# Selective scans on one core: the first of four states scanned in PSUM and multiplied there by VectorE, the other three by GpSimd a step later

## The chip, the core and the metric

The kernel runs on 1 core of one Trainium2 chip. It uses the core's five engines: TensorE (PE in the profile; PEld is its loading of weights), VectorE (DVE), ScalarE (ACT), GpSimd (POOL) and SyncE (SP, which here only issues DMAs). Each engine works through its own queue in order and waits on semaphores that the others raise. VectorE, ScalarE and GpSimd read and write SBUF; VectorE and ScalarE also read and write PSUM, the banks that TensorE writes.

The metric is device time in microseconds. Before the change it was 11,709.09 us, the median of 3 runs (11,697.75 to 11,709.36).

## The reference, cut to what matters

The program is four layers over 4 images of 64 x 64 positions with 96 channels. Layers 0 and 1 are Mamba-like blocks: each image is read in four orders, and along each order a selective scan runs for every channel and each of 16 states. Layer 1 does this on a half spectrum (33 x 64 positions, Fourier transforms around it). Layers 2 and 3 are attention without softmax and a quantized feed-forward network on the tokens. What the change touches is the scan:

```
def step(hst, inputs):
    ul, dl, bl, cl = inputs
    dA = jnp.exp(dl[..., None] * A)
    hst = hst * dA + (dl * ul)[..., None] * bl[:, :, None, :]
    y = jnp.einsum('bkdn,bkn->bkd', hst, cl)
    return (hst, y)
```

So for each channel d and state n, along the sequence l: `h[l] = exp(delta[l] * A[n]) * h[l-1] + delta[l] * u[l] * B[n, l]`, and `y[l]` is the sum over the 16 states of `h[n, l] * C[n, l]`.

## The kernel before, in words

The scans are one long loop, written out by hand in `scans` (line 480): the kernel's text is the order of the instructions on PE, VectorE, ScalarE and GpSimd. There are six phases: two of layer 0 (two images each) and four of layer 1 (one image each). A phase has four directions, a direction is cut into segments of the sequence (eight of 512 in layer 0; 512, 512, 384, 384 and 320 in layer 1), 144 segments in all. A segment has 4 groups of states (`q`, four states each) times 3 chunks of 128 channels (`c`): 12 steps, 1,728 in all. A step treats 128 channels on the partitions, S positions along the free axis, and four states, of which 0 and 1 are called x and 2 and 3 are called y.

For a step the loop (lines 763 to 828) needs:
- the factors `exp(delta * A)` of four states, by ScalarE (line 635): of the x states into SBUF (`ax`), of the y states into a PSUM bank (`ay`, from `room`);
- the inputs `delta * u * B`. For the x states ScalarE makes them transposed, piece by piece, well ahead (`make_bx`, line 600), and TensorE transposes them into a PSUM bank (`px`, line 630). For the y states GpSimd multiplies `du` by the broadcast B into the SBUF tile `hy` (`front_b`, line 653), which has one buffer;
- four scans by VectorE (`scan`, line 660): x from SBUF and PSUM into the SBUF tile `hx`, y from PSUM and SBUF in place in `hy`;
- the products with C, two states at a time: GpSimd makes `hcx` (line 805), VectorE makes `hcy` (line 822);
- the last column of each state, copied into `state` for the next segment (`keep_state`, line 673): of x by GpSimd, of y by ScalarE (by GpSimd when ScalarE has a long burst);
- the sum over states: TensorE transposes the products into the accumulating bank `acc` (`accumulate`, line 682), two states at a time; after the last group ScalarE copies `acc` out and SP stores it (`close_chunk`, line 709).

Three PSUM banks with the tag `ab` serve `px` and `ay` in rotation, in the order in which `room` is called. B and C come as rows of a DRAM tensor `xd`, broadcast over the partitions by DMAs on SP's queue (`broadcast`, line 580; `fetch` gets one group `q` ahead, at `c == 0`): C in two tiles of two states with four buffers, B in one tile of two states with two buffers. In layer 0 each tile takes two DMAs, one per image.

Other work is threaded through the steps. `prepare` makes `delta`, `du` (line 560, one VectorE product of three chunks per segment), the transposes and `xd` for the next segment; an environment `E` works off side tasks of the other layers: projections with TensorE, flips with GpSimd (line 306), normalization and gating (line 440 is a VectorE product with two SBUF operands), tokens and their feed-forward network (lines 1133, 1211, 1230, 1234 on VectorE). Both advance in the `slot` calls, three a step; pieces marked `LATE` (mostly those with VectorE work) only in the last one, and long ScalarE pieces, marked `BURST`, only in `burst`.

## Time and profile before

| what | value | where from |
|---|---|---|
| median of 3 runs | 11,709.09 us | times |
| profiled execution: span | 11,704.4 us | head of the page (the page gives no other time of that execution) |
| before the first scan, after the last | 215 us, 396 us | timeline: the first scan starts at 215.5, the last ends at 11,308.3 |
| VectorE, ScalarE, GpSimd, PE busy | 90%, 78%, 76%, 79% | page, part 1 |
| four scans of a step of 512 | 4.8 us | timeline, start to start |
| `hcy`, 1024 elements | 1.311 us mean | groups by shape |
| `hcx`, 1024 / 768 / 640 elements | 2.363 / 1.818 / 1.545 us mean | groups by shape |
| one product of `front_b`, 512 / 384 / 320 | 1.272 / 0.999 / 0.862 us mean | groups by shape |
| state copy on GpSimd, two columns | 0.850 us mean | groups |
| DMA queues busy, mean over 16 engines | 45.5% | page, part 3 |

A row of a timeline reads: start and duration in us, engine, line of the kernel, operation, tiles written and read, shapes, and how many like it are merged; in brackets, how long the engine sat idle before it and what ended that. In rows of windows, each engine has its busy time in us and its number of instructions; the last three columns are the granted TensorE clock, the DMA engines' busy share and GB/s. Tile names lose their trailing digits, so `ab_l`, `b_l` and `_l` name the rotating PSUM banks.

### The profile page before, as it was taken

The numbers are of one execution on the slowest core, as the hardware profiler recorded it, in microseconds if no ns is written. First come the engines' busy times: TensorE is split into PE (matmuls) and PEld (weight loads), VectorE is DVE, ScalarE is ACT, GpSimd is POOL, SyncE is SP. The second block draws the span as 40 slices with busy tenths as digits, with TensorE's granted clock in tenths as the row PEclk, the third lists the DMA queues.
The fourth block names the chain that finished last, engine by engine and source line by source line (L and its number), as shares of the span: only waits on it lengthen the run. The fifth ranks groups of instructions, "written<-read, shape, count | busy, mean of one in ns | idle before, by whom it ended". The sixth has DMA issues, their size and how long they took to land. (4 is left out here: it accounts for less than half of the span.)

```text
span 11704.4 us, 164864 instructions
## 1 busy us (share of the span) xinstructions
PE 9301.7 (79%) x54800; PEld 6722.3 (57%) x54800; DVE 10549.4 (90%) x10183; ACT 9089.0 (78%) x18533; POOL 8931.5 (76%) x7075
## 2 busy tenths in 40 slices
PE   6678888787888878877888888888778877788765
PEld 3455555555666556555665565565556655565554
DVE  6899999999999998999888989988999999899974
ACT  3778888898888888887767878877787787777753
POOL 2889999887887897897768878877767767677640
PEclk8789999988988998998889989988879988898887
DMA  5454454555555445445544353454225432443242
GB/s 145 120 142 119 126 127 115 141 155 158 153 153 129 124 124 141 120 127 162 153 129 124 114 147 120 142 150 119 88 79 158 122 96 92 124 137 106 83 117 42
DMA packets 1270879, 1469.07 MB, mean 126 GB/s; under 512 B 496071, under 2 KB 1033871, under 8 KB 1260679
## 3 DMA queue, kind: packets, MB, share of 16 engines
q1 hardware_dynamic: 1270023, 1458.53, 45.5%
q8 instruction: 430, 7.05, 0.3%
q14 instruction: 426, 3.49, 0.1%
HBM read 1221.74 MB, written 236.50 MB: 125 GB/s over the span
## 5 line engine op out<-in xcount | busy, mean ns | idle before, releaser
L653 POOL TENSOR_TENSOR hy_l<-du_l,bc_l 128x512 f32<-128x512 f32 (+2 forms) x3456 | 3957.3, 1166 | 1934.8 <-DVE hcy_l L822 960.1
L805 POOL TENSOR_TENSOR hcx_l<-hx_l,bc_l 128x1024 f32<-128x1024 f32 (+2 forms) x1617 | 3525.5, 2180 | 239.1 <-DVE hx_l L660 197.9
L600 ACT ACTIVATE bx_l<-dut_l,bt_l 128x192 f32<-128x192 f32 (+2 forms) x6272 | 2793.7, 498 | 0.0
L682 PE MATMUL acc_l<-ident,hcx_l 128*128 128x128 f32 (+1 forms) x12006 | 1876.0, 305 | 392.6 <-POOL hcx_l L805 388.4
L635 ACT ACTIVATE ax_l<-delta_l,l_alog 128x512 f32<-128x512 f32 (+2 forms) x3456 | 2139.1, 667 | 0.0
L682 PE MATMUL acc_l<-ident,hcy_l 128*128 128x128 f32 (+1 forms) x12000 | 1841.9, 302 | 302.4 <-DVE hcy_l L822 299.0
L682 PEld LDWEIGHTS acc_l<-ident,hcy_l 128*128 128x128 f32 (+1 forms) x12000 | 1551.5, 155 | 859.2 <-DVE hcy_l L822 475.7
L682 PEld LDWEIGHTS acc_l<-ident,hcx_l 128*128 128x128 f32 (+1 forms) x12006 | 1526.4, 156 | 861.5 <-POOL hcx_l L805 665.9
L822 DVE TENSOR_TENSOR hcy_l<-hy_l,bc_l 128x1024 f32<-128x1024 f32 (+2 forms) x1616 | 1951.1, 1207 | 43.6
L660 DVE TENSOR_TENSOR_SCAN hx_l<-ax_l,state_l,b_l 128x512 f32<-128x512 f32 (+2 forms) x1650 | 1787.4, 1124 | 212.7 <-PE b_l L630 136.9
L660 DVE TENSOR_TENSOR_SCAN hy_l<-b_l,state_l,hy_l 128x512 f32<-128x512 f32 (+2 forms) x1649 | 1782.9, 1118 | 89.3 <-ACT b_l L635 81.4
L635 ACT ACTIVATE b_l<-delta_l,l_alog 128x512 f32<-128x512 f32 (+2 forms) x1913 | 1196.6, 628 | 627.6 <-DVE hx_l L660 599.0
L630 PE MATMUL b_l<-ident,bx_l 128*128 128x128 f32 (+1 forms) x6724 | 1169.6, 302 | 363.0 <-DVE hy_l L660 203.5
L635 ACT ACTIVATE ab_l<-delta_l,l_alog 128x512 f32<-128x512 f32 x1321 | 907.1, 689 | 547.5 <-DVE hx_l L660 496.4
L630 PEld LDWEIGHTS b_l<-ident,bx_l 128*128 128x128 f32 (+1 forms) x6724 | 827.1, 152 | 861.3 <-DVE hy_l L660 337.1
L660 DVE TENSOR_TENSOR_SCAN hy_l<-ab_l,state_l,hy_l 128x512 f32<-128x512 f32 x961 | 1172.1, 1257 | 60.8 <-POOL hy_l L653 31.9
L660 DVE TENSOR_TENSOR_SCAN hx_l<-ax_l,state_l,ab_l 128x512 f32<-128x512 f32 x962 | 1176.5, 1263 | 49.3 <-PE ab_l L630 27.3
L630 PE MATMUL ab_l<-ident,bx_l 128*128 128x128 f32 x5288 | 889.1, 305 | 383.2 <-DVE hy_l L660 206.3
L673 POOL COPY state_l<-hx_l 128x2 f32<-128x2 f32 x1344 | 1141.9, 850 | 0.0
L630 PEld LDWEIGHTS ab_l<-ident,bx_l 128*128 128x128 f32 x5288 | 652.0, 154 | 715.6 <-DVE hy_l L660 326.6
L274 PE MATMUL pc_l<-pad_l,l_dg 128*128 128x512 f32 (+2 forms) x1656 | 787.9, 564 | 56.0 <-ACT uh_l L252 46.6
L176 PE MATMUL pi_l<-xi_l,l_wi 96*128 96x384 f32 (+6 forms) x912 | 458.6, 619 | 180.0 <-ACT zh_l L342 60.4
(225 smaller groups left out, 11821.3 us busy)
## 6 DMA issues: line engine op xcount, KB each, us to landing
bc_l<-l_xd_l SPq DMA_DIRECT2D x1536, 256.0 KB
bc_l<-l_xd_l SPq DMA_DIRECT2D x384, 512.0 KB
bc_l<-l_xd_l SPq DMA_DIRECT2D x384, 384.0 KB
us_l<-l_u SPq DMA_DIRECT2D x96, 768.0 KB
l_y<-y_l SPq DMA_DIRECT2D x288, 256.0 KB
bc_l<-l_xd_l SPq DMA_DIRECT2D x192, 320.0 KB
yt_l<-l_y SPq DMA_DIRECT2D x264, 192.0 KB
yt_l<-l_y SPq DMA_DIRECT2D x128, 384.0 KB
```

The lines of the kernel that those rows point to most:

```text
L176: self.nc.tensor.matmul(out[i * cfg.PI : (i + 1) * cfg.PI, :n], wi[:, ki, half, :], xin[:, max(i, ki), :n], start=(ki == 0), stop=(ki == c ...
L274: nc.tensor.matmul(pc[:, : n * 64].rearrange("p (r w) -> p r w", w=64), diag[:, t, :], pad[:, r - p0 + dy : r - p0 + dy + n, dx : dx + 64] ...
L600: nc.scalar.activation(t[:n, b, :, ch], z.dut[:n, b, :, ch], AF.Copy, scale=z.bt[:n, b, m : m + 1])
L630: nc.tensor.transpose(pb[:, t : t + n], st.z.bx[st.q, j][:n, b, st.c], ident[:n, :n])
L635: nc.scalar.activation(out, z.delta[:, st.c, : z.S], AF.Exp, scale=z.blk.A[:, st.c, z.k, n : n + 1])
L653: nc.gpsimd.tensor_tensor(st.hy[:, j, :S], st.z.du[:, st.c, :S], st.z.b[st.q][:, j, :S], ALU.mult)
L660: nc.vector.tensor_tensor_scan(h[:, j, : z.S][:, ::step], a[:, : z.S][:, ::step], b[:, : z.S][:, ::step], 0.0 if z.first else z.state[st.c ...
L673: copy(z.state[st.c][:, n0 : n0 + 2].rearrange("p (j o) -> p j o", o=1), h[:, :, e : e + 1])
L682: nc.tensor.matmul(z.acc[st.c][:n, b, :], hc[:, j, t : t + n], ident, start=(n0 + j == 0 and b == 0), stop=(n0 + j == NST - 1 and b == 0), ...
L805: nc.gpsimd.tensor_tensor(hcx[:, :, :S], hx[:, :, :S], z.c[q][0][:, :, :S], ALU.mult)
L822: nc.vector.tensor_tensor(hcy[:, :, :S], st.hy[:, :, :S], z.c[q][1][:, :, :S], ALU.mult)
```

## The change

A step keeps its four scans, but the results go to other places and the products are shared out differently.
- State 0 is scanned in place in its PSUM bank `px[0]`. VectorE multiplies it with C right after, from PSUM into a new SBUF tile `hk` (512 elements); ScalarE copies its last column from PSUM; TensorE adds it to `acc` in the same step (`multiply_kept`).
- States 1, 2 and 3 are scanned into one SBUF tile `h` of three rows with three buffers. In the next step, GpSimd copies their last columns (one copy of three) and multiplies all three rows by C in place (`multiply`); TensorE adds them to `acc` in that next step, behind its transposes for the step after (`add_rest`).
- `hcx`, `hcy`, `hx` and `hy` go. `front_b` for the next step now stands in GpSimd's queue behind `multiply` for the previous one.
- The exponentials of states 2 and 3 are both issued within their own step, so that the PSUM banks rotate in another order.
- B is fetched at `c == 0` as before; C is fetched at `c == 1` instead, as one tile of four rows with two buffers (the same bytes in half the DMAs).
- `acc` is taken when its first product comes, `close_chunk` runs one step later, and a new phase's side tasks are added at its third step instead of its first.

```
+        self.kept = 1
+        self.px, self.ay = {}, {}
...
-        t = sp.tile([P, 2, SM], F32, name=f"bc{what}_{z.nm}_{n}", tag=f"bc{what}", bufs=2 + 2 * what)
+        t = sp.tile([P, many, SM], F32, name=f"bc{what}_{z.nm}_{n}", tag=f"bc{what}", bufs=2)
...
-    def fetch(z, q):
-        z.c[q] = [broadcast(z, 4 * q + 2 * j, 1) for j in range(2)]
-        z.b[q] = broadcast(z, 4 * q + 2, 0)
+    def fetch_b(z, q):
+        z.b[q] = broadcast(z, 4 * q + 2, 2, 0)
+
+    def fetch_c(z, q):
+        z.c[q] = broadcast(z, 4 * q, 4, 1)
...
-        st.hy = sp.tile([P, 2, SM], F32, name=f"hy_{st.nm}", tag="hy")
+        st.h = sp.tile([P, 3, SM], F32, name=f"h_{st.nm}", tag="h", bufs=3)
...
-    def scan(st, h, j, a, b, n):
+    def scan(st, j):
         z = st.z
-        step = -1 if z.rev else 1
+        S, step, n = z.S, -1 if z.rev else 1, 4 * st.q + j
+        h = st.px[j][:, :S] if j < st.kept else st.h[:, j - 1, :S]
+        a = st.ax[:, j, :S] if j < 2 else st.ay[j][:, :S]
+        b = st.px[j][:, :S] if j < 2 else h
...
+    def multiply_kept(st, j):
+
         z = st.z
+        n = 4 * st.q + j
+        hk = sp.tile([P, SM], F32, name=f"hk_{st.nm}_{j}", tag="hk", bufs=2)
+        nc.vector.tensor_tensor(hk[:, : z.S], st.px[j][:, : z.S], z.c[st.q][:, j, : z.S], ALU.mult)
         if not z.last:
+            e = last(z)
+            nc.scalar.copy(z.state[st.c][:, n : n + 1], st.px[j][:, e : e + 1])
+        accumulate(st, hk, n)
+
+    def multiply(st):
+
+        z = st.z
+        lo, n = st.kept - 1, 4 * st.q
+        h = st.h[:, lo:, : z.S]
+        if not z.last:
+            e = last(z)
+            nc.gpsimd.tensor_copy(
+                z.state[st.c][:, n + st.kept : n + 4].rearrange("p (j o) -> p j o", o=1), h[:, :, e : e + 1]
             )
+        nc.gpsimd.tensor_tensor(h, h, z.c[st.q][:, st.kept :, : z.S], ALU.mult)
...
+    def add_rest(st):
+        for j in range(st.kept, 4):
+            accumulate(st, st.h[:, j - 1], 4 * st.q + j)
...
-            hx = sp.tile([P, 2, SM], F32, name=f"hx_{st.nm}", tag="hx")
-            scan(st, hx, 0, st.ax[:, 0], st.px[0], 4 * q)
-            front_y(st, 1)
+            if c == 1:
+                if q + 1 < NQ:
+                    fetch_c(z, q + 1)
+                elif after:
+                    fetch_c(after, 0)
+            scan(st, 0)
+            front_y(st, 2)
             if nxt:
-                nxt.ay = {}
                 front_x(nxt)
+            multiply_kept(st, 0)
+            front_y(st, 3)
             long = burst()
-            scan(st, hx, 1, st.ax[:, 1], st.px[1], 4 * q + 1)
+            if before:
+                multiply(before)
+            if nxt:
+                front_b(nxt)
             slot(None)
+            scan(st, 1)
...
-                nxt.px = [transposed(nxt, 0)]
-            hcx = sp.tile([P, 2, SM], F32, name=f"hcx_{st.nm}", tag="hcx", bufs=2)
-            nc.gpsimd.tensor_tensor(hcx[:, :, :S], hx[:, :, :S], z.c[q][0][:, :, :S], ALU.mult)
-            keep_state(nc.gpsimd.tensor_copy, st, hx, 4 * q)
+                transposed(nxt, 0)
             more.take(skip=long)
-            scan(st, st.hy, 0, st.ay[0], st.hy[:, 0], 4 * q + 2)
+            scan(st, 2)
+            slot(None, hold=long)
             if nxt:
-                nxt.px.append(transposed(nxt, 1))
-            slot(None, hold=long)
-            scan(st, st.hy, 1, st.ay[1], st.hy[:, 1], 4 * q + 3)
-            keep_state(nc.gpsimd.tensor_copy if long else nc.scalar.copy, st, st.hy, 4 * q + 2)
-            if nxt:
-                front_y(nxt, 0)
-            more.take(skip=long and c == C - 1)
+                transposed(nxt, 1)
             if closing:
                 close_chunk(closing)
-            accumulate(st, hcx, 4 * q)
+            closing = None
+            if before:
+                add_rest(before)
+                closing = before if before.q == NQ - 1 else None
+            scan(st, 3)
+            more.take(skip=long and c == C - 1)
             slot(LATE)
-            hcy = sp.tile([P, 2, SM], F32, name=f"hcy_{st.nm}", tag="hcy", bufs=2)
-            nc.vector.tensor_tensor(hcy[:, :, :S], st.hy[:, :, :S], z.c[q][1][:, :, :S], ALU.mult)
-            if nxt:
-                front_b(nxt)
-            accumulate(st, hcy, 4 * q + 2)
-            closing = st if q == NQ - 1 else None
+            before = st
```

## The prediction

> **What bounds the kernel now.** I read the head of the page first, then the busy times by stage, the timeline of one step, and the groups by shape. PE is TensorE, DVE VectorE, ACT ScalarE, POOL GpSimd.
>
> ```profile
> span 11704.4 us, 164864 instructions
> PE 9301.7 (79%) x54800; PEld 6722.3 (57%) x54800; DVE 10549.4 (90%) x10183; ACT 9089.0 (78%) x18533; POOL 8931.5 (76%) x7075
> ...
> 215.00:2767.00 2552.00, 1967.03 (x10847) 1356.30 (x10847) 2419.91 (x1992) 2168.24 (x4486) 2264.40 (x1643) 0.89 0.50 130
> 2767.00:5353.00 2586.00, 2099.21 (x12844) 1592.02 (x12843) 2436.35 (x2041) 2179.46 (x4537) 2213.66 (x1598) 0.90 0.53 137
> 5353.00:6823.00 1470.00, 1251.74 (x7299) 917.10 (x7298) 1306.77 (x1310) 1105.06 (x2120) 1142.68 (x968) 0.88 0.48 138
> 6823.00:8270.00 1447.00, 1236.57 (x7383) 882.46 (x7382) 1295.60 (x1303) 1124.74 (x2186) 1146.69 (x975) 0.90 0.46 131
> 8270.00:9791.00 1521.00, 1200.79 (x7235) 873.21 (x7233) 1425.94 (x1576) 1176.99 (x2429) 1079.85 (x932) 0.86 0.36 107
> 9791.00:11308.00 1517.00, 1184.66 (x7255) 869.31 (x7253) 1410.42 (x1555) 1155.70 (x2376) 1076.32 (x932) 0.86 0.36 105
> ```
>
> The six rows are the six phases of scans (I call them A to F; columns: length, then PE, weight loads, VectorE, ScalarE, GpSimd busy). Together 11,093 us; 215 us before and 396 us after are untouched. VectorE is 89 to 95% busy in every one: it bounds. A step shows why:
>
> ```profile
> 3013.48 1.22 DVE L822 TENSOR_TENSOR hcy_l<-hy_l,bc_l 128x1024 f32<-128x1024 f32 x1
> 3014.78 2.45 DVE L660 TENSOR_TENSOR_SCAN hx_l<-ax_l,state_l,b_l 128x512 f32<-128x512 f32 x2
> 3017.15 2.43 DVE L660 TENSOR_TENSOR_SCAN hy_l<-b_l,state_l,hy_l 128x512 f32<-128x512 f32 x2
> 3019.62 1.22 DVE L822 TENSOR_TENSOR hcy_l<-hy_l,bc_l 128x1024 f32<-128x1024 f32 x1
> ...
> 3001.12 0.20 POOL L673 COPY state_l<-hx_l 128x2 f32<-128x2 f32 x1
> ...
> 3013.53 1.21 POOL L673 COPY state_l<-hx_l 128x2 f32<-128x2 f32 x1
> 3014.85 2.51 POOL L653 TENSOR_TENSOR hy_l<-du_l,bc_l 128x512 f32<-128x512 f32 x2
> 3017.38 2.36 POOL L805 TENSOR_TENSOR hcx_l<-hx_l,bc_l 128x1024 f32<-128x1024 f32 x1
> 3019.68 1.21 POOL L673 COPY state_l<-hx_l 128x2 f32<-128x2 f32 x1
> ```
>
> A step of 512 lasts 3019.62 − 3013.48 = 6.14 us: four scans and `hcy` back to back. GpSimd looks as full, but is not: its copy of two columns takes 0.20 us at 3001 and 1.21 us whenever `hcy` runs beside it, and ends with it. So while VectorE reads two operands from SBUF, GpSimd stands still. The scans, with one operand in PSUM, don't do that: `hcx` takes its 2.36 us under them. The reverse holds too:
>
> ```profile
> 5007.58 2.22 DVE L560 TENSOR_TENSOR du_l<-delta_l,us_l 128x1536 f32<-128x1536 f32 x1
> ...
> 5005.83 2.35 POOL L805 TENSOR_TENSOR hcx_l<-hx_l,bc_l 128x1024 f32<-128x1024 f32 x1
> 5008.13 1.72 POOL L673 COPY state_l<-hx_l 128x2 f32<-128x2 f32 x1
> ```
>
> `du` (1.73 us elsewhere) waits here until `hcx` ends at 5008.18, and the copy then waits for `du`.
>
> **The change, part by part.**
>
> *VectorE.* `hcy` goes (mean 1.311 us at 1024 elements, 0.996 at 768, 0.856 at 640). A product with one PSUM operand comes: the row of line 421 is the same form, 0.673, 0.542 and 0.474 us for 512, 384 and 320. Saved per step: 0.638, 0.454, 0.382 us. Each phase A, B has 384 steps of 512: 245 us; each of C to F has 96, 96, 48 steps of the three sizes: 61 + 44 + 18 = 123 us. If every stall of before stays, the VectorE path is A 2307, B 2341, C 1347, D 1324, E 1398, F 1394.
>
> *The scan that writes PSUM.* No row has VectorE writing PSUM. The nearest rows read it: scans with the PSUM operand first or second take 1.257 and 1.264 us, and adding a PSUM operand takes 0.539 us (line 1193) where the same add in SBUF takes 0.555 (line 1234). Bounds: −0.02 us, and +1.26 us (the whole scan again, if reading and writing one bank take turns). I take 0, from the nearer rows. [...]
>
> *GpSimd.* `hcx` becomes one product of 1536 elements in place. From 1.272 us (512) and 2.363 us (1024) each further 512 cost 1.091: 3.454 us, 3.39 start to start. The two products for B stay, 2.46 start to start. The copy, now three columns and with no `hcy` beside it, 0.12. Sum 5.97 us a step of 512; the same way 4.62 (384) and 3.93 (320). In place and with three rows I take as free; bounds −0 and +0.2 us (a copy's time) a step. By phase, with the flips of line 306 (0.62 us each) and the two-operand work of VectorE during which GpSimd stands (du 1.73, line 440 0.74, the token work): A 2292 + 60 + 55 = 2407; B 2292 + 31 + 55 + 18 = 2396; C 1206 + 29 + 15 + 17 = 1267; D 1264; E and F 1206 + 29 + 9 + 73 = 1317. So GpSimd becomes the bound in A and B, VectorE stays it in C to F.
>
> [...]
>
> *New wait: VectorE behind the long product.* A two-operand VectorE instruction now meets GpSimd in an instruction of 3.4 us. Per phase: du 32 times in A and B, 20 in C to F; line 440's group 0, 8, 8, 5, 5, 5; in E and F about 70 groups of token work each. Price between 0 and 3.4 us; the product fills half of GpSimd's step, so I take half of it, 1.7. What is queued behind on VectorE is the next scan, and behind that TensorE's transposes. A: 54 us, within the 100 us between VectorE path and GpSimd. B: 68 against 55. C 48, D 43, E and F 162. VectorE's old idle time (C 163, D 151, E 95, F 107) absorbs some, since PE and ACT catch up meanwhile; I let half of it do so: C and D 0, E and F about +115.
>
> *Moved.* GpSimd's product waits for the last scan of the step before, and in front of it in the queue nothing else waits; B's products follow and have a third buffer, so they no longer wait for `hcy` (960 us of GpSimd idle in the waits). TensorE's 12 matmuls wait for the product; behind them stand the next 4 and a group of transposes, at 0.13 us a matmul and 0.66 a group some 2.7 us, needed 3.8 us after the product ends when GpSimd leads by a step: free, and with side work up to 1 us late, which VectorE's 0.5 us a step takes back over two steps. ScalarE's copy of one column (0.19) replaces one of two columns. SP's queue issues 4 DMAs for C and B instead of 6 (some 0.5 us each less), but C a step later and after the product of GpSimd: C and B land 9 us after issue (2009 to 2018 in the DMA share) and have some 11 us instead of 18. Free, with the loads and stores behind C waiting no longer than now.
>
> Sum: A 2450 and B 2445 (40 to 50 us for starts and the handing over between the two engines), C 1347, D 1324, E 1513, F 1509: 10,588, with 611 outside 11,199. The page gives this execution's span alone; it lies 5 us under the median of 11,709. So about 11,200 us, 4.3% less.
>
> **The rivals.**
> 1. Everything overlaps: each phase at its larger floor, 10,266 + 611 + 5 = 10,880. For it: third buffer, slack on VectorE. Against: the old stalls come from PE and ACT.
> 2. The port decides (slower side). Place: the groups of two-operand VectorE work at lines 440, 1211, 1230 and du in C to F, 28 + 25 + 95 + 95 = 243 occasions. If each pays the whole 3.4 us and nothing absorbs it, 826 us come on top of 10,880, plus 90 in A and B: about 11,800, slower. At 2.5 us it is 11,580; it passes the time before at about 3.0. For it: these groups start right after the last scan, just as GpSimd's product does. Against: at 11192.92 a copy on GpSimd waited 3.23 us through du and `hcy` together, so VectorE can keep the port through a row of instructions.
> 3. The in-place scan is slow. From +0.64 us a step VectorE is where it was; at +1.26 it adds some 0.6 × 1600 = 960: 12,700.
> 4. C comes late: 576 fetches (144 segments, four each). A wait of 0.2 to 1 us each gives 11,300 to 11,800; at 0.9 us the gain is gone. For it: the shorter window and GpSimd's product in front. Against: the DMA engines are busy 0.36 to 0.53 of the time.
>
> **How the numbers follow.** Forecast 0.55 (10,950 to 11,420); rival 1 0.13; rival 2 0.20 (11,420 to 11,850: 0.10 faster, 0.03 same, 0.07 slower); rival 3 0.05 (0.01 faster); rival 4 0.07 (0.04 faster, 0.01 same, 0.02 slower). Faster 0.83, same 0.04 (within 0.2%, about what this kernel's runs can tell), slower 0.13. From 10,850 to 11,650 leaves out about 0.06 below and 0.13 above.
>
> **What would show it.** GpSimd's product at 3.4 to 3.5 us and its copy at 0.2; GpSimd above 95% busy in A and B, and a step of 512 near 6.0 to 6.1 us there; VectorE's product near 0.67 and its first scan at 1.26; du longer than 1.9 us on average. Wrong if the first scan takes over 1.5 us, the product over 3.7, VectorE idles on DMA for C, or du and line 1211 wait the whole product.

## The result, and the profile after

The changed kernel takes 12,155.5 us (median of 4 runs, 12,143.9 to 12,164.2) where the kernel before takes 11,709.2 (median of 4): a ratio of 1.0375, 95% interval 1.0359 to 1.039. It is 446 us slower; 11,200 was forecast. The head of the page after:

```profile
span 12147.2 us, 162665 instructions
PE 9149.4 (75%) x54800; PEld 6816.5 (56%) x54800; DVE 10278.3 (85%) x10183; ACT 9049.7 (75%) x18688; POOL 9954.7 (82%) x6920
```

VectorE is busy for 271 us less than before, as if a part of the saving had come, GpSimd for 1,023 us more. The six phases A to F, as rows of windows cut at their first scans (length, then PE, weight loads, VectorE, ScalarE, GpSimd busy):

```profile
214.80:2780.70 2565.90, 1896.33 (x10829) 1384.12 (x10830) 2267.64 (x1992) 2141.26 (x4526) 2411.04 (x1599) 0.89 0.52 130
2780.70:5400.30 2619.60, 2043.32 (x12851) 1594.41 (x12850) 2291.11 (x2041) 2158.31 (x4576) 2404.73 (x1561) 0.90 0.55 135
5400.30:6891.20 1490.90, 1230.17 (x7297) 916.19 (x7295) 1227.19 (x1310) 1102.27 (x2138) 1269.18 (x949) 0.88 0.45 136
6891.20:8381.20 1490.00, 1210.00 (x7382) 876.89 (x7382) 1229.85 (x1303) 1123.16 (x2209) 1269.87 (x953) 0.90 0.43 127
8381.20:10071.90 1690.70, 1215.32 (x7236) 913.33 (x7235) 1510.69 (x1578) 1184.91 (x2447) 1299.70 (x917) 0.81 0.32 97
10071.90:11746.40 1674.50, 1193.13 (x7271) 900.23 (x7269) 1495.67 (x1557) 1159.76 (x2392) 1286.91 (x914) 0.83 0.31 95
```

A to D are 14 to 43 us longer than before, E and F 169 and 158. The granted TensorE clock (third column from the end) is 0.81 and 0.83 in E and F, against 0.86 before; TensorE's busy time there rises by 14 and 8 us only, so a slower TensorE doesn't explain these two phases. The rows add up to 11,532 us, 439 more than before; outside the scans the time is the same (616 us against 611). VectorE's busy time in the phases falls from 10,295 to 10,022, its idle time rises from 798 to 1,509.

A step that nothing disturbs is as short on VectorE as forecast. Timeline of the changed kernel, VectorE and GpSimd:

```profile
3030.06 1.26 DVE L666 TENSOR_TENSOR_SCAN b_l<-ax_l,state_l,b_l 128x512 f32<-128x512 f32 x1
3030.42 0.20 POOL L696 COPY state_l<-h_l 128x3 f32<-128x3 f32 x1
...
3030.70 3.45 POOL L699 TENSOR_TENSOR h_l<-h_l,bc_l 128x1536 f32<-128x1536 f32 x1
...
3031.36 0.69 DVE L683 TENSOR_TENSOR k_l<-b_l,bc_l 128x512 f32<-128x512 f32 x1
...
3034.11 2.51 POOL L656 TENSOR_TENSOR h_l<-du_l,bc_l 128x512 f32<-128x512 f32 x2
...
3035.51 1.26 DVE L666 TENSOR_TENSOR_SCAN b_l<-ax_l,state_l,b_l 128x512 f32<-128x512 f32 x1
...
3036.83 3.47 POOL L699 TENSOR_TENSOR h_l<-h_l,bc_l 128x1536 f32<-128x1536 f32 x1
```

From first scan to first scan VectorE needs 3035.51 − 3030.06 = 5.45 us (6.14 before), GpSimd from product to product 3036.83 − 3030.70 = 6.13 us. So in such steps VectorE runs ahead until it has to wait, and GpSimd goes on without a break. What that does to a VectorE instruction with two SBUF operands is seen elsewhere in the same kernel. The usual case:

```profile
944.52 4.11 DVE L562 TENSOR_TENSOR du_l<-delta_l,us_l 128x1536 f32<-128x1536 f32 x1
...
943.56 3.46 POOL L699 TENSOR_TENSOR h_l<-h_l,bc_l 128x1536 f32<-128x1536 f32 x1
946.96 4.04 POOL L656 TENSOR_TENSOR h_l<-du_l,bc_l 128x512 f32<-128x512 f32 x2
```

`du`, 1.73 us of work, waits until GpSimd's product ends at 947.02; then it goes first, and GpSimd's next two products take 4.04 us, not 2.51. The worst case:

```profile
1480.73 13.73 DVE L562 TENSOR_TENSOR du_l<-delta_l,us_l 128x1536 f32<-128x1536 f32 x1
...
1480.01 3.46 POOL L699 TENSOR_TENSOR h_l<-h_l,bc_l 128x1536 f32<-128x1536 f32 x1
1483.40 2.52 POOL L656 TENSOR_TENSOR h_l<-du_l,bc_l 128x512 f32<-128x512 f32 x2
1485.84 0.63 POOL L306 COPY ut_l<-uh_l 128x256 f32<-128x256 f32 x1
1486.41 3.44 POOL L699 TENSOR_TENSOR h_l<-h_l,bc_l 128x1536 f32<-128x1536 f32 x1
1489.79 2.50 POOL L656 TENSOR_TENSOR h_l<-du_l,bc_l 128x512 f32<-128x512 f32 x2
1492.21 0.63 POOL L306 COPY ut_l<-uh_l 128x256 f32<-128x256 f32 x1
```

Here `du` takes 13.73: it gets nowhere until GpSimd, after eight instructions in a row, has nothing more to do at 1492.84. Of the 96 `du` of this size, 50 took longer than 2.5 us, and seven longer than 8; the next longest took 4.65. Of the 73 that waited for more than 0.2 us, 66 waited for one GpSimd instruction, and the seven for four to eight. The seven are each the `du` of a direction's first segment; what makes them different is not settled. Their waiting is 65 of the 155 us that these 96 waited.

In the kernel before, the same `du` met a GpSimd that stood still or was about to (timeline of the kernel before):

```profile
2990.38 0.19 POOL L673 COPY state_l<-hx_l 128x2 f32<-128x2 f32 x1
2996.36 2.50 POOL L653 TENSOR_TENSOR hy_l<-du_l,bc_l 128x512 f32<-128x512 f32 x2 [5.80 <-DVE hcy_l L822]
...
2993.35 1.73 DVE L560 TENSOR_TENSOR du_l<-delta_l,us_l 128x1536 f32<-128x1536 f32 x1
2995.00 1.22 DVE L822 TENSOR_TENSOR hcy_l<-hy_l,bc_l 128x1024 f32<-128x1024 f32 x1
```

There GpSimd waits 5.80 us for `hcy`, because `hy` has one buffer, and the late side work of VectorE lies just in that pause. Not every `du` found GpSimd idle: 58 of the 96 started with more than 0.2 us of a GpSimd instruction left, mostly of `hcx`. But behind that stood only the small state copy, which the `du` of the prediction's second timeline passed, and then the wait: `du` took 1.96 us on average and 2.69 at most. This wait was GpSimd's largest before; the change took it away. The row of it in GpSimd's waits before (us in total, times, longest):

```profile
POOL hy_l L653 <- DVE hcy_l L822: 960.1, 530, 10.6
```

And the two largest of GpSimd's waits after:

```profile
POOL state_l L696 <- DVE h_l L666: 614.2, 318, 12.1
POOL h_l L656 <- PE acc_l L709: 449.1, 235, 13.0
```

### The profile page after: what moved, and what is told of

The parts are those of the page before. It is cut to its first block, busy times and chain, and to the rows that moved or that the text cites. A ratio compares the mean times of both kernels' runs of the same rounds, so it can differ in the third digit from the quotient of the medians.

```text
span 12147.2 us, 162665 instructions
## 1 busy us (share of the span) xinstructions
PE 9149.4 (75%) x54800; PEld 6816.5 (56%) x54800; DVE 10278.3 (85%) x10183; ACT 9049.7 (75%) x18688; POOL 9954.7 (82%) x6920
## 5 line engine op out<-in xcount | busy, mean ns | idle before, releaser
L699 POOL TENSOR_TENSOR h_l<-h_l,bc_l 128x1536 f32<-128x1536 f32 (+2 forms) x1728 | 5450.1, 3154 | 384.5 <-DVE h_l L666 261.2
L656 POOL TENSOR_TENSOR h_l<-du_l,bc_l 128x512 f32<-128x512 f32 (+2 forms) x3456 | 4134.2, 1218 | 555.5 <-PE acc_l L709 449.1
L709 PE MATMUL acc_l<-ident,h_l 128*128 128x128 f32 (+1 forms) x19008 | 2788.9, 303 | 503.3 <-POOL h_l L699 501.8
L709 PEld LDWEIGHTS acc_l<-ident,h_l 128*128 128x128 f32 (+1 forms) x19008 | 2473.7, 158 | 619.1 <-POOL h_l L699 598.0
L666 DVE TENSOR_TENSOR_SCAN h_l<-b_l,state_l,h_l 128x512 f32<-128x512 f32 (+2 forms) x1688 | 1839.0, 1119 | 253.3 <-ACT b_l L638 219.0
L666 DVE TENSOR_TENSOR_SCAN h_l<-ab_l,state_l,h_l 128x512 f32<-128x512 f32 x1024 | 1263.3, 1264 | 154.2 <-ACT ab_l L638 100.0
L666 DVE TENSOR_TENSOR_SCAN b_l<-ax_l,state_l,b_l 128x512 f32<-128x512 f32 (+2 forms) x843 | 951.6, 1129 | 322.1 <-PE b_l L634 320.1
L666 DVE TENSOR_TENSOR_SCAN h_l<-ax_l,state_l,b_l 128x512 f32<-128x512 f32 (+2 forms) x843 | 949.1, 1126 | 81.7 <-PE b_l L634 79.8
L709 PE MATMUL acc_l<-ident,k_l 128*128 128x128 f32 (+1 forms) x3400 | 614.6, 302 | 512.4 <-DVE k_l L683 500.3
L696 POOL COPY state_l<-h_l 128x3 f32<-128x3 f32 x1392 | 357.0, 256 | 619.2 <-DVE h_l L666 614.2
L666 DVE TENSOR_TENSOR_SCAN ab_l<-ax_l,state_l,ab_l 128x512 f32<-128x512 f32 x513 | 653.3, 1273 | 156.5 <-PE ab_l L634 155.8
```

The lines of the kernel that those rows point to most:

```text
L656: nc.gpsimd.tensor_tensor(st.h[:, 1 + j, :S], st.z.du[:, st.c, :S], st.z.b[st.q][:, j, :S], ALU.mult)
L666: nc.vector.tensor_tensor_scan(h[:, ::step], a[:, ::step], b[:, ::step], 0.0 if z.first else z.state[st.c][:, n : n + 1], ALU.mult, ALU.add,)
L696: nc.gpsimd.tensor_copy(z.state[st.c][:, n + st.kept : n + 4].rearrange("p (j o) -> p j o", o=1), h[:, :, e : e + 1])
L699: nc.gpsimd.tensor_tensor(h, h, z.c[st.q][:, st.kept :, : z.S], ALU.mult)
L709: nc.tensor.matmul(z.acc[st.c][:m, b, :], hc[:, t : t + m], ident, start=(n == 0 and b == 0), stop=(n == NST - 1 and b == 0), is_transpose ...
```

## The experiments

All on the chip, each timed against the kernel before. Lengths of the phases in us, cut at the first scans:

| kernel | median us | A | B | C | D | E | F |
|---|---|---|---|---|---|---|---|
| before | 11,709 | 2552 | 2586 | 1470 | 1447 | 1522 | 1517 |
| changed | 12,155 | 2566 | 2620 | 1491 | 1490 | 1691 | 1675 |
| before, without GpSimd's product | 11,431 | 2443 | 2493 | 1442 | 1422 | 1508 | 1503 |
| changed, without GpSimd's product | 11,270 | 2347 | 2464 | 1422 | 1422 | 1509 | 1499 |
| changed, `du` with a PSUM operand | 11,997 | 2508 | 2565 | 1484 | 1471 | 1684 | 1669 |
| changed, three short products | 12,123 | 2643 | 2671 | 1497 | 1498 | 1605 | 1590 |
| changed, product of two rows | 11,615 | 2391 | 2521 | 1444 | 1455 | 1603 | 1591 |
| changed, one input product | 11,726 | 2381 | 2511 | 1452 | 1454 | 1662 | 1653 |
| before, two buffers for `hy` | 12,113 | 2567 | 2643 | 1510 | 1489 | 1646 | 1641 |

### What GpSimd's product costs, in both kernels

The long product left out of the changed kernel, and `hcx` left out of the kernel before:

```
-        nc.gpsimd.tensor_tensor(h, h, z.c[st.q][:, st.kept :, : z.S], ALU.mult)
```
```
-            hx = sp.tile([P, 2, SM], F32, name=f"hx_{st.nm}", tag="hx")
+            hx = sp.tile([P, 2, SM], F32, name=f"hx_{st.nm}", tag="hx", bufs=2)
-            nc.gpsimd.tensor_tensor(hcx[:, :, :S], hx[:, :, :S], z.c[q][0][:, :, :S], ALU.mult)
-            accumulate(st, hcx, 4 * q)
+            accumulate(st, hx, 4 * q)
```

> Leaves out: GpSimd's product of states 1 to 3 with C (the copy of their last columns stays). Three theories of where the time went. PORT: VectorE's instructions with two SBUF operands (du, the gating, the token work) wait behind GpSimd's 3.45 us product; that is 568 us more of VectorE busy time. QUEUES: TensorE stands in order behind that product and behind VectorE's new product, and ScalarE behind TensorE and VectorE; that is 736 us more of VectorE idle time. SUM: GpSimd's own 6.13 us a step is simply the bound. All three say that without the product the rest runs as the prediction had it for VectorE: about 2,310, 2,340, 1,345, 1,325, 1,400, 1,395 us in phases A to F, 10,750 in all (10,600 to 11,000). If it stays above 11,400, none of the three is the main cause: then the new order itself (PSUM banks in another rotation, exponentials and accumulation moved) costs the time.

> The kernel before (11,704), with GpSimd's product of states 0 and 1 left out (TensorE adds the scans' results themselves; their tile has two buffers). In the changed kernel leaving out GpSimd's product took 885 us. If it was the product's port that cost VectorE in both kernels, about 885 x 2/3 = 590 goes here too: 11,100 to 11,250. If before's order kept VectorE's operations with two SBUF operands out of GpSimd's way (GpSimd's next products wait for VectorE's own product, and the late side work stands right before that), little goes: 11,500 to 11,700.

Measured: 11,270.0 (ratio 0.9629, 0.961 to 0.9648) and 11,430.5 (0.9763, 0.9744 to 0.9782). So the product costs 885 us in the changed kernel and 277 before, three times as much for 1.5 times the elements; and all the rest of the change is a gain of 160 us: 885 − 277 − 160 = 448, which is the loss but for 2 us (each run is set against the kernel before as timed beside it). Two things follow. Most of the loss hangs on the product. And VectorE's saving hardly counts: without products VectorE is busy for 9,429 us after and 10,066 before, 637 less, and gains 160, of which 125 lie in A and B. In D, E and F the two kernels are equal to within 5 us.

### Queues and loads: what the change did not make worse

The waits of the changed kernel had many new entries, so the first suspects were its queues. TensorE's waits after:

```profile
PE acc_l L709 <- POOL h_l L699: 501.8, 350, 9.1
PE acc_l L709 <- DVE k_l L683: 500.3, 242, 9.6
PE acc_l L709 <- DVE hk_l L683: 472.6, 192, 10.9
```

First, TensorE adds states 1 to 3 two steps later instead of one, so that it needn't wait for GpSimd's product (`h` gets a fourth buffer, for which `hk` and `xs` give one up):

```
-            if before:
-                add_rest(before)
-                closing = before if before.q == NQ - 1 else None
+            if older:
+                add_rest(older)
             scan(st, 3)
...
+            older, before = before, st
```

> Nothing is left out: TensorE adds states 1 to 3 two steps later instead of one (four buffers for h; one for hk and xs to make room). Then the product has long been done when TensorE comes to it. QUEUES: TensorE's 500 us of idle time behind GpSimd's product go, ScalarE's waits for the transposes of du fall from 552 towards 200 us, VectorE's idle time falls by 200 to 300: about 11,900. PORT and SUM: VectorE still waits for the port and GpSimd for its own work: 12,100 to 12,200.

Measured: 12,344.1 (1.0548, 1.0532 to 1.0564), slower than the changed kernel. TensorE's wait for the product was gone from its list; its waits for VectorE's product grew to 585 + 572 us. The buffers given up may have a part in that, so the run gives no sign that this wait was the cause, and doesn't rule it out.

Next, TensorE adds state 0 behind its transposes:

```
-        accumulate(st, hk, n)
+        st.hk[j] = hk
...
+            for j in st.hk:
+                accumulate(st, st.hk[j], 4 * q + j)
             if before:
                 add_rest(before)
```

> Only the place of one group of instructions changes: TensorE adds VectorE's product of state 0 to acc behind its transposes for the next step, instead of right after the product was issued, so that side work and transposes no longer stand behind it in TensorE's queue. Changed kernel 12,155. QUEUE (TensorE's 1,055 us of waits for VectorE's product are what makes the transposes late): the waits go, VectorE's idle time on TensorE falls from 745 toward before's 303, and the whole comes to 11,700 to 11,850. PLACE DOES NOT MATTER (TensorE waits in one place what it does not wait in another): 12,100 to 12,200. In between would mean that a part of it counts.

Measured: 12,156.1 (1.0377, 1.0361 to 1.0392), no change at all. TensorE waits for the scans in place of the products:

```profile
PE b_l L634 <- DVE h_l L666: 728.5, 494, 7.0
PE ab_l L634 <- DVE h_l L666: 653.5, 414, 9.1
```

In the changed kernel TensorE waited 1,055 us for VectorE's product (two rows of its list above and 82 us in a third); these are gone, the two rows shown grew by 725 (from 366 and 291), and the time stood still. So these waits look like a result of VectorE being late, not its cause.

ScalarE's copy of state 0's last column (which waited 674 us for VectorE's product) left out, alone and with the edit above. The scan of state 0 then starts from 0 in every segment:

```
-            0.0 if z.first else z.state[st.c][:, n : n + 1],
+            0.0 if z.first or j < st.kept else z.state[st.c][:, n : n + 1],
...
-            nc.scalar.copy(z.state[st.c][:, n : n + 1], st.px[j][:, e : e + 1])
```

> Left out: ScalarE's copy of the last column of state 0 (each segment's state 0 starts from 0; the three other states are carried on). It takes away 1,440 copies of 0.15 us, 215 us of ScalarE, and the 674 us that ScalarE waited before them for VectorE's product. COPY (ScalarE's waiting there makes the exponentials late): VectorE's idle time on ScalarE falls from 450 toward before's 180, the whole comes to 11,850 to 11,950. BANK (the next exponential goes into the same PSUM bank and waits for the same product anyway): 12,080 to 12,160, and the wait shows at that exponential.

> The two edits together: TensorE's add of state 0 behind the transposes, and ScalarE's copy of state 0 left out. If both queues cost and on their own: 11,450 to 11,650. If only TensorE's: about as with that edit alone, within 50. If neither: 12,050 to 12,200, and the rest of the loss lies in VectorE's waits for the GpSimd product and in that product's length.

Measured: 12,034.2 (1.0271, 1.0254 to 1.0287) and 12,030.9 (1.0268, 1.0252 to 1.0284). 121 us for 215 us of ScalarE taken away, and again nothing from TensorE's place. But a scan of 512 in PSUM that starts from a constant takes 1.213 us instead of 1.273, and VectorE's busy time in the phases falls by 94 us with it, so how much of the 121 is the copy's isn't shown. The wait moved to the exponential that reuses the bank (ScalarE on VectorE's products, 521 + 498 us), as the expectation BANK said; the gain lies between the two expectations.

The exponential of state 2 put back to where the kernel before had it:

```
-            front_y(st, 2)
...
             scan(st, 3)
+            if nxt:
+                front_y(nxt, 2)
```

> One part of the change undone: ScalarE's exponential of state 2 for the next step is issued right behind the last scan of this step, ahead of the late side work, as the kernel before did with its first y state; the order in which the PSUM banks are taken stays. Changed kernel 12,155. LOOKAHEAD (exponentials issued just in time turn each late ScalarE into VectorE's waiting): VectorE's idle time on ScalarE falls from 450 toward before's 180, the whole comes to 11,850 to 11,950. LOAD (ScalarE has no time to spare where VectorE waits for it, wherever the exponential stands): 12,080 to 12,200.

Measured: 12,129.4 (1.0361, 1.0336 to 1.0387). 26 us.

A quarter of all exponentials left out, in both kernels:

```
-        for j in range(2):
-            exp(st.ax[:, j, : st.z.S], st, 4 * st.q + j)
+        exp(st.ax[:, 0, : st.z.S], st, 4 * st.q)
...
```

> The changed kernel with 1,728 of ScalarE's 6,912 exponentials left out (state 1 takes the factors of state 0, which lie in SBUF): about 1,000 us of ScalarE. LOAD (with VectorE's step at 5.45 us ScalarE's side work has become as long as the steps it lies in, so the steps of the new kernel end on ScalarE and TensorE's chain): the time falls by 300 to 500, to 11,650 to 11,850. PORT AND GPSIMD (GpSimd's 6.1 us a step and its port hold): it falls by less than 150.

> The same exponentials left out of the kernel before (11,705), as the measure for the other run. LOAD, where ScalarE had slack before and has none after: this one falls by less than half of what the changed kernel loses, 11,500 to 11,650. If ScalarE counts alike in both, the two falls agree within 50 us, and ScalarE is not what the change made worse.

Measured: 11,991.9 (1.0243, 1.0222 to 1.0264), 164 us less than the changed kernel, and 11,589.3 (0.9902, 0.9879 to 0.9924), 120 less than the kernel before. ScalarE counts nearly alike in both. A fourth PSUM bank for inputs and factors, in both (chunks 1 and 2 are summed into one bank, so that their sums come out mixed; the changed kernel also adds state 0 behind the transposes, which alone changed nothing):

```
-        return ps.tile([P, 512], F32, name=f"ab_{st.nm}_{j}", tag="ab", bufs=3)
+        return ps.tile([P, 512], F32, name=f"ab_{st.nm}_{j}", tag="ab", bufs=4)
...
+        if n == 0 and st.c == 2:
+            z.acc[2] = z.acc[1]
```

> A fourth PSUM bank for the inputs and factors of the scans, in the changed kernel. The bank is won by summing chunks 1 and 2 into one bank, so the sums of these two chunks come out mixed; the number of adds and copies is the same. TensorE's adds of state 0 stand behind its transposes, as in the run where that changed nothing (12,156). SLACK (each bank is refilled with 1.6 to 2.5 us to spare in a step of 5.45 us, and any later transpose or exponential becomes VectorE's waiting): VectorE's idle time falls from 1,510 to about 1,000, the whole comes to 11,600 to 11,800. NOT THE BANKS (the producers are late for their own queues' sake): 12,080 to 12,200.

> The same fourth bank, won in the same way, in the kernel before (11,708). SLACK: before had 1.9 to 2.9 us to spare for each refill and 690 us of idle time on VectorE; it gains less, 11,500 to 11,680. NOT THE BANKS: 11,680 to 11,730. If both kernels gain the same, the banks are not what the change made worse.

Measured: 11,992.3 (1.0243, 1.0226 to 1.0261) and 11,569.3 (0.988, 0.9859 to 0.99): 163 and 138 us. The banks too are worth something in both kernels, and are not what the change made worse.

### How long VectorE waits: du and the length of the instruction

`du` with one operand in PSUM (TensorE copies `u` there; the first chunk's `u` serves all three chunks):

```
+        nc.tensor.matmul(pu[:, :S], ident, u[:, 0, :S], start=True, stop=True)
...
-        nc.vector.tensor_tensor(z.du[:, :, :S], z.delta[:, :, :S], u[:, :, :S], ALU.mult)
+        nc.vector.tensor_tensor(z.du[:, :, :S], z.delta[:, :, :S], pu1, ALU.mult)
```

> Leaves out: the product du takes u of chunk 0, put into a PSUM bank by one matmul, for all three chunks; sizes stay. [...] PORT: du goes from a mean of 2.6 us back to 1.8, and the two dear steps of a segment (the eighth and tenth) shrink: A from 2,566 to about 2,450, B from 2,620 to about 2,510, C to F 20 to 40 each; in all about 11,850. QUEUES: VectorE's du gets shorter by 130 us in sum, but the waits behind it stay: about 12,030. SUM: A is at GpSimd's 2,411 of work in 2,566 already: at most 60 us in A, about 12,050 in all.

Measured: 11,996.6 (1.025, 1.0233 to 1.0268), 159 us less. The 96 largest `du`, in the changed kernel and in this one (groups by shape; busy us, mean ns). First the changed kernel:

```profile
L562 DVE TENSOR_TENSOR du_l<-delta_l,us_l 128x1536 f32<-128x1536 f32 x96 | 321.5, 3349 | 37.1 <-ACT delta_l L546 37.1
```

With the operand in PSUM:

```profile
L565 DVE TENSOR_TENSOR du_l<-delta_l,pp_l 128x1536 f32<-128x1536 f32 x96 | 165.8, 1728 | 38.9 <-PE pp_l L560 38.9
```

The same product with one operand in PSUM waits for nobody: 1.72 to 1.75 us every time. All `du` together take 171 us less and the kernel gains 159. That is one instruction per segment, and a third of the loss (in the kernel before, `du` waits for 31 us in all).

GpSimd's product cut into three instructions of one row:

```
+        for j in range(st.kept, 4):
+            hj = st.h[:, j - 1, : z.S]
+            nc.gpsimd.tensor_tensor(hj, hj, z.c[st.q][:, j, : z.S], ALU.mult)
```

> Nothing is left out: GpSimd's product is issued as three of 512 instead of one of 1536, 0.3 us more of GpSimd time a step (about 480 us over 1,728 steps), but VectorE has to wait for 1.27 us at most. PORT: E and F lose about 100 us each, C and D 20 to 40, while A and B (GpSimd near its bound) gain up to 100 each: about 12,050 (11,950 to 12,200), and line 1245 comes down from 1.0 us mean towards 0.5. QUEUES: TensorE may start after the first third, which takes some of its 500 us behind the product away: about 12,000. SUM: 0.3 us a step wherever GpSimd is the bound: 12,400 to 12,600.

Measured: 12,122.9 (1.0357, 1.0342 to 1.0373). Inside it lie two opposite moves: E and F fall by 86 and 85, as the expectation had it for VectorE's token work, which now meets instructions of 1.302 us, not 3.468 (how long that work took in this run isn't shown); A and B rise by 77 and 51, where GpSimd's sum of a step is the longest and its work grows (three rows take 3 x 1.302 us instead of 3.468).

### GpSimd's sum of a step

Two runs shorten GpSimd's sum. One multiplies two rows, not three (state 3 without its C); the other leaves out `front_b`'s input product for state 3, and leaves the long product as it is:

```
-        nc.gpsimd.tensor_tensor(h, h, z.c[st.q][:, st.kept :, : z.S], ALU.mult)
+        h2 = st.h[:, lo:2, : z.S]
+        nc.gpsimd.tensor_tensor(h2, h2, z.c[st.q][:, st.kept : 3, : z.S], ALU.mult)
```
```
-        for j in range(2):
+        for j in range(1):
             nc.gpsimd.tensor_tensor(
                 st.h[:, 1 + j, :S], st.z.du[:, st.c, :S], st.z.b[st.q][:, j, :S], ALU.mult
...
-        b = st.px[j][:, :S] if j < 2 else h
+        b = st.px[j][:, :S] if j < 2 else h if j < 3 else z.du[:, st.c, :S]
```

> GpSimd's product cut to two rows of 512 (2.4 us in place of 3.45; state 3 is added without its C). GpSimd's sum of a step becomes 5.1 us, below VectorE's 5.45. PORT (the cost goes with the time for which GpSimd works beside VectorE): 12,155 - 885/3 = 11,860. LENGTH (GpSimd's sum above VectorE's is what holds the steps up): it falls to the price that such a product has in the kernel before, 11,270 + 277 = 11,550, or up to 11,650.

> The changed kernel without GpSimd's product of the input of state 3 (that scan takes du itself, so B is left out for it). GpSimd's sum of a step falls from 6.13 to 4.86 us, its long product of 3.45 us stays. LENGTH (the steps are held up because GpSimd's sum exceeds VectorE's 5.45, and VectorE's two-operand operations find no pause): 11,550 to 11,750, and du takes less than 2 us again in most places. HOLD (VectorE waits for the one long instruction, whatever GpSimd's sum): 11,950 to 12,150, and du keeps most of its waiting.

Measured: 11,614.9 (0.992, 0.9903 to 0.9937), 540 us less than the changed kernel, and 11,726.4 (1.0024, 1.0014 to 1.0034), 429 less. A third of the product carries 540 of its 885 us, and half as much as the product costs comes back when the product isn't touched at all. In the changed kernel GpSimd's sum of a step, 6.13 us, lies above VectorE's 5.45; in these two runs it lies below, by an estimate from measured durations (with `hcx` of the kernel before for two rows 6.13 − 3.47 + 2.36 = 5.0, without an input product 6.13 − 1.27 = 4.9). Whether the gain comes where one passes the other was not measured, and a shorter sum is not enough by itself (the last experiment below). `du` with one input product and with the long product still there:

```profile
L562 DVE TENSOR_TENSOR du_l<-delta_l,us_l 128x1536 f32<-128x1536 f32 x96 | 169.0, 1761 | 37.1 <-ACT delta_l L546 37.1
```

1.76 us: in most steps GpSimd now stands still, waiting for the last scan (before its state copy 1,192 times and 1,746.6 us, in the changed kernel 318 times and 614.2 us), and `du`, which is issued right behind that scan, goes first. GpSimd had more than 0.2 us of an instruction left at the start of 11 of these 96 `du`, of 77 in the changed kernel. Phases A and E of this run:

```profile
217.30:2598.50 2381.20, 1823.85 (x10829) 1326.89 (x10830) 2169.95 (x1992) 2132.30 (x4526) 1957.23 (x1216) 0.92 0.56 140
...
8015.40:9677.50 1662.10, 1204.65 (x7235) 905.83 (x7234) 1488.40 (x1577) 1182.62 (x2447) 1023.28 (x676) 0.83 0.32 98
```

A comes within 34 us of its length without the product (2347); E doesn't (1509): its VectorE is busy for 1,488 us against 1,340 there. So in A and B it is mostly GpSimd's length, in E and F mostly the long instruction itself: line 1245 of the token work takes 1.000 us on average here, 1.087 in the changed kernel and 0.350 without the product. Of the 885 us, 429 go when GpSimd's sum is shortened, and 456 stay with the product, 307 of these in E and F (1,662 − 1,509 and 1,653 − 1,499).

### The pause, taken away from the kernel before

If VectorE's late work was quick because GpSimd stood still beside it, then a second buffer for `hy` must slow the kernel before, though it removes 960 us of waiting (`hcx` gives up one of its two buffers for it):

```
-        st.hy = sp.tile([P, 2, SM], F32, name=f"hy_{st.nm}", tag="hy")
+        st.hy = sp.tile([P, 2, SM], F32, name=f"hy_{st.nm}", tag="hy", bufs=2)
...
-            hcx = sp.tile([P, 2, SM], F32, name=f"hcx_{st.nm}", tag="hcx", bufs=2)
+            hcx = sp.tile([P, 2, SM], F32, name=f"hcx_{st.nm}", tag="hcx", bufs=1)
```

> The kernel before (11,708), with two buffers for hy, so that GpSimd's input products for the next step need not wait until VectorE's product of this step is done (hcx has one buffer instead of two, to make room). PAUSE (in the kernel before, GpSimd stood still while VectorE did du, the late side work and its own product): these operations now meet GpSimd's, hcy grows beyond 1.31 us and du beyond 1.96, and the whole comes to 11,780 to 12,000. NO PAUSE NEEDED: the freed GpSimd changes nothing or helps, 11,600 to 11,715.

Measured: 12,112.6 (1.0354, 1.0339 to 1.037), 415 us slower than the kernel before, nearly the loss of the whole change. It all shows on VectorE: busy for 10,730 us in the phases against 10,295, idle for 766 against 798. GpSimd's idle time hardly falls (2,014 us in the phases after 2,169); it stands still at another place, before `hcx`. First the row of the kernel before, then of this run:

```profile
POOL hcx_l L805 <- DVE hx_l L660: 197.9, 145, 8.8
...
POOL hcx_l L805 <- DVE hx_l L660: 1149.2, 815, 10.2
```

The groups of this run that grew, `hcy` and two of the token work:

```profile
L822 DVE TENSOR_TENSOR hcy_l<-hy_l,bc_l 128x1024 f32<-128x1024 f32 x1152 | 1653.4, 1435 | 32.2
...
L1211 DVE TENSOR_SCALAR h<-h,b 128x512 f16<-128x512 f16 x192 | 102.2, 572 | 11.3 <-ACT h L1208 7.9
...
L1234 DVE TENSOR_TENSOR tok<-tok,y 128x384 f32<-128x384 f32 x64 | 71.0, 1112 | 1.7
```

Before they took 1.311, 0.377 and 0.555 us on average. By their durations VectorE's instructions grew by 239 us in `hcy`, by 173 in the side work (149 of them in E and F) and by 13 in `du`, which took 2.08 us, not 1.96. So the pause was worth this much to the kernel before, but more than half of it to `hcy`, which the changed kernel no longer has: the 415 us can't be carried over to the changed kernel as they stand. The edit slows E and F by 124 each, where the change costs 169 and 158, and A by 15, where the change costs 14; why A is spared here isn't shown.

### Sharing the products out otherwise

VectorE keeps two states in PSUM in every second step, so that GpSimd multiplies two rows and three in turn; then the same with the fourth bank:

```
-        self.kept = 1
+        self.kept = 1 + (C * q + c) % 2
```

> One size changed: in every second step VectorE keeps two states in PSUM (states 0 and 1) and GpSimd multiplies two rows, not three. By the rows: VectorE +554 of products, GpSimd's products -950, so that GpSimd's sum of a step of 512 goes from 6.13 to 5.6 us on average and VectorE's from 5.45 to 5.8. GPSIMD'S LENGTH (its sum and its hold of the port set the time): 11,850 to 12,000. VECTORE (what is added to it is added to the time): 12,350 to 12,600. Where both balance: about 12,150.

> The kernel in which VectorE keeps two states in every second step (12,265), with the fourth bank (chunks 1 and 2 summed into one bank). There the loads are level (phase A: VectorE 2,315, GpSimd about 2,250 of 2,588 us) and still the steps are long. SLACK: it gains most here, since a kept state holds its bank for 0.7 us more: 11,600 to 11,850. NOT THE BANKS: 12,150 to 12,300.

Measured: 12,264.5 (1.0476, 1.0455 to 1.0497) and 11,978.2 (1.0227, 1.0207 to 1.0247). In the first, GpSimd's length falls and `du` takes less (63 us in phase A, not 138), but VectorE is back at 10,299 us of busy time in the phases, with 1,346 us idle; so GpSimd's sum below VectorE's does not by itself make the kernel fast. The bank is worth 286 us here, against 163 and 138 elsewhere (the second run also adds the kept states behind the transposes); that a kept state holds its bank for one product more (0.692 us) fits this, and wasn't tried by itself. No kernel of this study that computes everything is faster than the one before.

## Why the prediction was wrong

By its own steps, against the 10,588 us that it summed for the phases and the 11,532 measured:

- **Durations and floors: right.** GpSimd's product took 3.468 us (3.454 forecast), its copy 0.2, VectorE's product 0.692 (0.673). From start to start the copy costs 0.27 us, not 0.12, so that GpSimd's step took 6.13 us, not 5.97. GpSimd's floors were forecast as 2407, 2396, 1267, 1264, 1317, 1317 and measured as 2411, 2405, 1269, 1270, 1300, 1287. But A and B didn't run at that floor: GpSimd was busy for 94% and 92% of them, not above 95%, and they took 116 and 175 us more than the sum said.
- **The scan that writes PSUM: right.** 1.273 us against 1.264; rival 3 is out. `du` took 1.728 us with an operand in PSUM and 1.73, undisturbed, with both in SBUF.
- **C a step later: right.** VectorE's waits for the DMA of C came to a few us; rival 4 is out.
- **"If every stall of before stays": wrong, 551 us.** That was the path of VectorE with its products alone, 10,111 us. Without GpSimd's product the phases took 10,662, with VectorE idle for 1,233 us where the kernel before had 798. A quicker VectorE waits longer: over the span 734 us behind TensorE and 604 behind ScalarE, where the kernel before without its product has 476 and 397. Three quarters of the saving went there. What holds D to F at the same length in both kernels without products is not settled: queue places, the exponential's place, ScalarE's load and the banks were tried, with the product in place, and each counted little or about as much in both.
- **"New wait: VectorE behind the long product": the wait was right, its absorption wrong; 392 us with GpSimd's bound in A and B.** The sum put 477 us on top of VectorE's path: 247 in A and B, where GpSimd's floor was to be the bound, nothing in C and D, and 230 in E and F. The product put 869 on it: 375, 136 and 358. Of these 593 are waiting inside VectorE's instructions, near the 537 forecast before anything was absorbed; in C to F it is 414 us over the 243 occasions counted, 1.7 us each, as forecast. The step that failed is "I let half of it do so": VectorE's idle time absorbed nothing and grew by 276 us. The bound of one GpSimd instruction held for 66 of the 73 `du` that waited; seven waited through four to eight, 65 us in all.
- **"Moved": free. Wrong.** The prediction named GpSimd's 960 us of waiting for `hcy` and counted its end as harmless. It was the cover of VectorE's late work; ended by itself, in the kernel before, it costs 415 us (239 of VectorE's growth there in `hcy`). In the changed kernel a shorter GpSimd sum, with GpSimd standing still again in most steps, gives 429 us back. What share of the 446 us is due to the lost pause alone isn't shown. GpSimd's sum above VectorE's, which the prediction took as a floor beside others, means that few other pauses take its place: GpSimd is idle for 370 of the 5,186 us of A and B.

Rival 1, everything overlapping, fell with the last three points. Rival 2, VectorE's two-operand work waiting at GpSimd's product, had the right cause and side (what it and the expectations call the port no run shows as such; shown are the waits, as of `du` until 947.02, and that with an operand in PSUM `du` takes 1.728 us), and its 11,800 was still too low, although it priced the wait at 826 us: it stacked that on a floor that held the full saving, and did not count that VectorE's idle time would grow.

## What to carry to other kernels

Before you remove a wait of an engine, look at what the other engines do during it; a pause that a single buffer forces on GpSimd can be what lets VectorE's SBUF work through (here its end cost the kernel before 415 us). When work goes to GpSimd, add up its sum of a step against VectorE's, not only against its own idle time: where GpSimd became the longer here, 6.13 us against 5.45, it seldom stood still, and of the 73 `du` that waited, with two SBUF operands each, 66 waited for the GpSimd instruction under way and seven for four to eight. An undisturbed step that gets shorter promises nothing for a loop whose average step is set by side work; measure first what is left of the saving, here a quarter, by taking the new cost out altogether.

## What was not expected of the hardware

- A VectorE instruction waited through many GpSimd instructions, not only the one under way: `du` at 1480.73 through eight, four others through six (12.07, 12.06, 11.18, 10.63 us). This was rare, seven of the 73 `du` that waited; the 66 others went on after one, and these seven didn't get their turn there.
- It wasn't only instructions with two SBUF tensors that grew: line 1245, 16-bit with a bias per partition, went from a mean of 0.377 us (line 1211 of the kernel before) to 1.087, and line 1248, a cast from f16 to fp8, from 0.959 (line 1214) to 1.499. Without GpSimd's product they take 0.350 and 1.021 in the changed kernel. The rows of the changed kernel:

```profile
L1245 DVE TENSOR_SCALAR h<-h,b 128x512 f16<-128x512 f16 x192 | 200.6, 1087 | 11.8 <-ACT h L1242 8.5
...
L1248 DVE CAST h<-h 128x1536 fp8e5<-128x1536 f16 x64 | 95.6, 1499 | 1.8
```
